# A cross-attention and feed-forward kernel: its first block in two halves, its opening reordered, the last values in row pairs

## The chip, the cores and the metric

One core of one Trainium2 chip. A core has a matrix engine (TensorE, PE in the profile, its weight loads PEld), a vector engine (VectorE, DVE), a scalar engine (ScalarE, ACT), a general engine (GpSimd, POOL), a queue engine (SyncE, SP), and 16 DMA engines that they share. Each engine works through its own instructions in the order of the program and waits for the others by semaphores. The metric is the device time of one execution, in microseconds (us).

## What is computed

x is 2048 rows of 256, the context 1601 rows of 192, all in float32. The rows of x are normalised, attend to the context with 16 heads of 64 (a learned null key and value stand ahead of the 1601), are projected back, normalised and added; then a feed-forward network of three layers with weights of +1 and -1 is added.

```python
def attention(x, context, mask):
    x = layer_norm(x, g_norm)
    q = x @ Wq
    k, v = jnp.split(context @ Wkv, 2, axis=-1)
    q, k, v = (to_heads(q), to_heads(k), to_heads(v))
    k = jnp.concatenate([nk, k], axis=2)
    v = jnp.concatenate([nv, v], axis=2)
    sim = jnp.einsum('bhid,bhjd->bhij', q * sqrt_scale, k * sqrt_scale)
    sim = jnp.where(full_mask, sim, max_neg)
    out = jnp.einsum('bhij,bhjd->bhid', softmax(sim), v)
    return layer_norm(merge_heads(out) @ Wout, g_out)

x = x + attention(_layernorm(x), ctx_768, mask)
x = x + ffn(_layernorm(x), k0, k1, k2, s0, s1, s2)
```

## The kernel before

**Tiling.** The rows of x are four blocks of 512 (b), each four tiles of 128; the heads are eight pairs (p), so that a pair fills 128 partitions. The 1602 keys are 13 tiles of 128 (KC), in four chunks for the maxima: 512, 512, 512 and 66 (CHUNKS). There are 32 units (p, b), counted u from 0. All of the program is under a manual schedule: what each engine does follows the order of the calls.

**A unit.** For each of the 13 key tiles, TensorE makes transposed scores (L442), ScalarE their exponents (L468), GpSimd adds the exponents up into acc (L720 to L728), and, for the unit after this one, TensorE makes untransposed scores (L400, L384) of which VectorE takes row maxima (L403, L387). Then come the products with the values (L475), the last unit's output projection, the queries of the unit after next (project_q), and one part of the next pair's keys (project_k, b = 0 and 1) or values (project_v, b = 2 and 3). A softmax shift, the maximum, is put into the scores by one matmul (L466) for the first two key tiles of a unit.

**Values.** A values block is up to eight key tiles in one PSUM tile of two banks, four tiles of 128 columns to a bank. values_begun (L300) multiplies the first 128 of the context's 192 rows (ctx_a), values_ended (L314) adds the other 64 (ctx_b). ctx_b and the weights wb hold these 64 rows twice, in partitions 0 to 63 and 64 to 127, so that two matmuls with 64 rows each can lie in the array at once: a tile in the first bank takes the lower rows, one in the second bank the upper. Block m = 0 holds tiles 0 to 7, block m = 1 tiles 8 to 12: 8 to 11 in the first bank, 12 in the second. values_ended goes through the tiles so that those with the same place in the two banks follow each other: 8, 12, 9, 10, 11. One ScalarE copy (L329) takes the block to SBUF. The units do project_v(p, 1) for p = 1 to 7.

**The opening** (L579 to L677), before the first unit. Transfers are issued from three queues: GpSimd's (the identity is made first, then g_norm, null keys, the mask's row `keep`), SP's and ScalarE's (x in four tiles in turns, the first context chunk on ScalarE's, the weights of pair 0 and the rest on SP's). Then block 0 is normalised whole: statistics of four tiles (L79, L80), a root on ScalarE (L535), a reciprocal (L543), four centrings (L91) on VectorE; TensorE meanwhile does eleven matmuls of the identity with itself into a spare PSUM tile (L635), which are used for nothing. It transposes the block (L556, scaled into xnT by L557 and L561), makes the first 512 keys (first_keys(0), L243 with ctx_a and L250 with ctx_b; VectorE subtracts the null key and masks them, L232, and ScalarE and GpSimd round them to kr, L258 and L260) and the queries in two halves of 256 (first_queries, L226 to L228). From there maxima of block 0 (max_chunk, twelve of 512 keys and REST for the last 66 of all four tiles), the other keys and the values of pair 0, the normalisation of block 1 (second_summed, second_normed, input_turned(1)) and its queries (project_q(0, 1)) are woven together. The opening ends with the first scores, the shifts (max_combined, max_turned) and a count of masked keys (masked_counted, L428) in front of the first L466.

PSUM is eight banks: two tiles of two banks each in a pool `flex` (ps_f) and two in a pool `spare` (ps_s). Calls for a tile take the two of a pool in turns and wait until the tile taken two calls before has been read.

**Two tiny copies** on ScalarE in each unit (`seen`, L708 and L711) read a value of the last exponents and of the last unit's acc, and so make ScalarE wait for those who write them. The second stands at step 8 of the 13, in units 3 to 27 at step 2:

```python
for k in range(KC):
    if k == (2 if 2 < u < len(units) - 4 else 8) and last is not None:
        nc.scalar.copy(seen[:, 1:2], last[3][:1, 0, 0:1])
```

Of the kernel before, what the change touches and what calls it, by code (L numbers as in the profile page):

```python
# [9 lines left out]
F32 = mybir.dt.float32  # L10
# [11 lines left out]
CD = 192  # L22
# [9 lines left out]
REST = 12  # L32
# [6 lines left out]
def xattn_ffn(ctx, tc, x, ctxT, mask, g_norm, null_kv, wq, wkv, wout, g_out, k0, k1, k2, s0, s1, s2, out):  # L39
# [55 lines left out]
    n_slots = 0  # L95
# [52 lines left out]
    with ExitStack() as att:  # L148
# [22 lines left out]
        def load_pair(p):  # L171
            wq_t = pp.tile([128, 2, 128], F32, tag="wq", name=f"wq_{p}")
            wa_t = pp.tile([128, 2, 128], F32, tag="wa", name=f"wa_{p}")
            wb_t = pp.tile([128, 2, 128], F32, tag="wb", name=f"wb_{p}")
            wo_t = lp.tile([128, D], F32, tag="wo", name=f"wo_{p}")
            both = wkv.rearrange("r (k w) -> r k w", k=2)[:, :, ts(p, 128)]
            nc.sync.dma_start(out=wa_t, in_=both[0:128])
            nc.sync.dma_start(out=wb_t[:64], in_=both[128:CD])
            nc.sync.dma_start(out=wb_t[64:], in_=both[128:CD])
            nc.sync.dma_start(out=wq_t, in_=wq[:, ts(p, 128)].rearrange("(c r) w -> r c w", c=2))  # L180
            if p > 0:
                nc.sync.dma_start(out=wo_t, in_=wout[ts(p, 128), :])
            weights[p] = (wq_t, wa_t, wb_t, wo_t)
# [32 lines left out]
        def first_queries(h):  # L216

            if h == 0:
                qT = wp.tile([128, 512], F32, tag="qT", name="qT_0_0")
                qr = wp.tile([128, 512], F32R, tag="qr", name="qr_0_0", bufs=1)  # L220
                queries[0, 0] = (qT, qr)
            qT, qr = queries[0, 0]
            ps = spare(f"psq_0_0_{h}")
            cols = ts(h, 256)
            for c in range(2):
                nc.tensor.matmul(ps[:, 0, :256], weights[0][0][:, c, :], xnT[:, 0, c, cols], start=c == 0, stop=c == 1)  # L226
            nc.scalar.mul(qr[:, cols], ps[:, 0, :256], DH**-0.5)  # L227
            nc.scalar.mul(qT[:, cols], ps[:, 0, :256], DH**-0.5)  # L228
# [5 lines left out]
        def first_keys(n, get, part=None):  # L234
# [3 lines left out]
            if part != 1:  # L238
                halves["k"] = get(f"psk_0_{n}")
# [6 lines left out]
            if part == 0:  # L246
                return
# [51 lines left out]

        def values_begun(p, m, tiles, get=flex):  # L300

            if (p, m) not in halves:
                halves[p, m] = get(f"psv_{p}_{m}").rearrange("p i (t d) -> p (i t) d", d=128)
            for t in tiles:
                nc.tensor.matmul(  # L305
                    halves[p, m][:, t - 8 * m, :],
                    ctx_a[:, ts(t, 128)],
                    weights[p][1][:, 1, :],
                    start=t % 4 == 0,
                    stop=False,  # L310
                    skip_group_check=True,
                )

        def values_ended(p, m):  # L314
# [3 lines left out]
            for t in sorted(tiles, key=lambda t: (t % 4, t)):  # L318
                rows = ts((t - 8 * m) // 4, 64)
                nc.tensor.matmul(  # L320
                    pv[:, t - 8 * m, :],
# [6 lines left out]
            w = len(tiles)  # L328
            nc.scalar.copy(v[:, ds(8 * m, w), :], pv[:, :w, :])  # L329
# [3 lines left out]
        def project_v(p, m):  # L333

            values_begun(p, m, range(8 * m, min(8 * m + 8, KC)))
            values_ended(p, m)

# [87 lines left out]
        def masked_counted(get):  # L425

            ps = get("count")
            nc.tensor.matmul(ps[:, 0, :KC], ones_r.bitcast(F32), kept, start=True, stop=True)  # L428
            nc.vector.tensor_reduce(spent, ps[:, 0, :KC], AX.X, ALU.add)
# [149 lines left out]
        nc.gpsimd.memset(keep[:, 0:1], 0)  # L579
        make_identity(nc, ident)  # L580
# [3 lines left out]
        nc.gpsimd.dma_start(out=keep[:, 1:], in_=mask.partition_broadcast(128))  # L584
        for t in range(4):
            (nc.sync, nc.scalar)[t % 2].dma_start(out=x_sb[:, t, :], in_=x[ts(t, 128), :])
        load_context(nc.scalar, 0)
        load_pair(0)
# [40 lines left out]
        xn = input_root(0)  # L629

        input_normed(0, *xn)

        idle = slot("idle")
        for _ in range(11):
            nc.tensor.matmul(idle[:, 0, :128], ident, ident, start=True, stop=True)  # L635
        input_turned(0, spare)
        first_keys(0, flex)
        first_queries(0)
        max_chunk(0, 0, 0)
        max_chunk(0, 0, 3)  # L640
        first_queries(1)
        nc.gpsimd.tensor_copy(kept[:, : KC - 1], mcol_u8[:, : KC - 1])
        nc.gpsimd.tensor_copy(kept[:KLAST, KC - 1 : KC], mcol_u8[:KLAST, KC - 1 : KC])
        mv, r = second_summed()
        max_chunk(0, 0, 6)
        first_keys(1, spare, 0)
        max_chunk(0, 0, 9)
        first_keys(1, spare, 1)
        values_begun(0, 0, range(0, 8), spare)
        max_chunk(0, 0, 1)  # L650
        nc.vector.reciprocal(r, r)
        second_normed(mv, r)
        nc.scalar.activation(warm, eps_sb, AF.Exp)
        max_chunk(0, 0, 4)
        values_ended(0, 0)
        max_chunk(0, 0, 7)
        first_keys(3, spare)
        max_chunk(0, 0, 10)
        values_begun(0, 1, range(8, KC), spare)
        max_chunk(0, 0, 2)  # L660
        values_ended(0, 1)
        max_chunk(0, 0, 5)
# [5 lines left out]
        max_chunk(0, 0, 11)  # L668
        project_q(0, 1, spare)
        max_chunk(0, 0, REST)  # L670
# [6 lines left out]
        masked_counted(flex)  # L677
        begin.__exit__(None, None, None)
        last = None
        with tc.manual_schedule():  # L680
            for u, (p, b) in enumerate(units):
# [27 lines left out]
                for k in range(KC):  # L709
                    if k == (2 if 2 < u < len(units) - 4 else 8) and last is not None:  # L710
# [243 lines left out]
```

## Time and profile before

| | us |
|---|---|
| median of 3 runs (lowest, highest) | 1270.21 (1269.99, 1270.72) |
| the profiled execution, its own time | 1270.18 |
| its span, first to last instruction | 1268.4 |
| TensorE busy | 1257.9 (99%) |
| VectorE, ScalarE, GpSimd busy | 761.7, 717.9, 1008.5 |
| opening, to the first exponent (L468) | 34.65 |
| units, from there to the last values' copy (L782) | 1079.25 - 34.65 = 1044.6 |
| feed-forward network after it | some 189 |

A profile lists what each engine did, by the line of the program that issued it. "Idle before" is the time that an engine stood still ahead of an instruction, with what released it. A matmul's end is modelled, so that those which follow each other overlap: the distance between starts tells more than the length. A float32 matmul is two instructions on TensorE. Transfers have a sequencer's time for the issue (SPq, ACTq) and a time to landing.

The engines' shares by slices of the span: TensorE is at nine tenths or more in nearly all of them, and transfers matter in the first slice alone:

```profile
PE   8999999999999999999999999999999999999998
PEld 5344444444444444444444444444444443788887
DVE  6687766656665566556655666656666793635431
ACT  4776666666666656665666566666666676322120
POOL 5898999899889988998899988998898999701100
PEclk9999999999999999999999999999999999999999
DMA  6000000000000000000000000000000010000000
```

### The profile page before, as it was taken

To read this page: it belongs to the slowest core of one execution; us is meant where nothing else is said; L and a number is where in the kernel's file an instruction comes from. 1 tells how busy PE (TensorE), PEld (TensorE's weight loads), DVE (VectorE), ACT (ScalarE), POOL (GpSimd) and SP (SyncE) were. 2 spreads that over 40 slices of the span, in tenths; PEclk is the share of its full clock that TensorE was granted. 3 is DMA by queue.
4 is the path that set the end of the run, shared out by engine and by line. 5 is a ranking of instruction groups with operands and counts; after the bars stand their busy time and mean duration, and the time that the engine had idled before them with its cause. 6 is when DMAs were issued, how large, how long until landed. Compare 5 with 4: busy or idle time off the path is not lost.

```text
span 1268.4 us, 19642 instructions
## 1 busy us (share of the span) xinstructions
PE 1257.9 (99%) x8332; PEld 644.0 (51%) x8332; DVE 761.7 (60%) x812; ACT 717.9 (57%) x982; POOL 1008.5 (80%) x515
## 2 busy tenths in 40 slices
PE   8999999999999999999999999999999999999998
PEld 5344444444444444444444444444444443788887
DVE  6687766656665566556655666656666793635431
ACT  4776666666666656665666566666666676322120
POOL 5898999899889988998899988998898999701100
PEclk9999999999999999999999999999999999999999
DMA  6000000000000000000000000000000010000000
GB/s 171 1 1 5 1 1 13 5 1 1 13 5 1 1 14 5 1 1 13 5 1 2 13 5 1 1 1 6 1 17 1 1 42 1 1 17 1 17 17 17
DMA packets 16984, 13.46 MB, mean 11 GB/s; under 512 B 3152, under 2 KB 16336, under 8 KB 16896
## 3 DMA queue, kind: packets, MB, share of 16 engines
q1 hardware_dynamic: 15904, 11.21, 3.2%
q8 instruction: 65, 1.06, 0.4%
q10 hardware_dynamic: 656, 0.79, 0.2%
q0 software_dynamic: 336, 0.21, 0.1%
q14 instruction: 23, 0.19, 0.0%
HBM read 10.11 MB, written 2.10 MB: 10 GB/s over the span
## 4 chain that ended last, share of the span: by engine, by line
PE 95%; POOL 2%; ACT 1%; DMA 1%; issue 0%; DVE 0%; SPq 0%; DVEq 0%; POOLq 0%; ACTq 0%
PE sT L442 28%; PE av L475 27%; PE ps L836 12%; PE max L400 7%; PE psq L211 4%; PE po L488 4%; PE ps L867 2%; PE psv L305 2%; PE psk L270 1%; PE den L499 1%; PE sT L466 1%; PE psv L320 1%; POOL acc L728 1%; PE psk L275 1%; PE max L384 1%; PE mt L413 1%
## 5 line engine op out<-in xcount | busy, mean ns | idle before, releaser
L403 DVE TENSOR_REDUCE mx<-max 128x2 f32<-128x1024 f32 x384 | 444.4, 1218 | 86.0 <-PE max L400 82.3
L728 POOL TENSOR_TENSOR acc<-acc,e 128x1024 f32<-128x1024 f32 x192 | 473.1, 2464 | 15.1
L468 ACT ACTIVATE e<-sT 128x1024 f32<-128x1024 f32 x416 | 425.8, 1024 | 87.7 <-PE sT L466 44.3
L442 PE MATMUL sT<-qT,kT 64*128 64x512 f32 x1664 | 444.8, 608 | 1.6 <-ACT e L468 1.3
L722 POOL TENSOR_TENSOR acc<-acc,e 128x1024 f32<-128x1024 f32 x160 | 379.3, 2371 | 12.6
L475 PE MATMUL av<-e,v 128*32 128x512 f32 x3328 | 363.6, 592 | 0.1
L400 PE MATMUL max<-kr,qr 64*128 64x512 f32 x768 | 280.6, 718 | 1.2 <-ACT qr L227 1.0
L475 PEld LDWEIGHTS av<-e,v 128*32 128x32 f32 x3328 | 107.4, 110 | 237.9 <-issue 230.1
L442 PEld LDWEIGHTS sT<-qT,kT 64*128 64x128 f32 x1664 | 134.0, 185 | 132.6 <-ACT e L468 121.0
L720 POOL TENSOR_TENSOR acc<-e,e 128x1024 f32<-128x1024 f32 x32 | 75.6, 2363 | 59.6 <-ACT e L468 59.6
L400 PEld LDWEIGHTS max<-kr,qr 64*128 64x128 f32 x768 | 76.7, 187 | 88.6 <-DVE mx L403 65.2
L517 ACT COPY aoT<-r 32x256 f32<-32x256 f32 x224 | 90.2, 403 | 33.4 <-DVE r L511 31.1
L782 ACT COPY avs<-av 128x512 f32<-128x512 f32 x32 | 18.8, 587 | 145.8 <-PE av L475 145.8
L415 DVE TENSOR_TENSOR mT<-mt,pick 128x512 fp32r<-128x512 f32 x32 | 22.1, 690 | 113.4 <-PE mt L413 112.9
L518 DVE TENSOR_TENSOR aoT<-avs,aoT 128x512 f32<-128x512 f32 x28 | 33.3, 1189 | 94.4 <-ACT aoT L517 94.4
L836 PE MATMUL ps<-h0hi,w 128*128 128x512 f32 x256 | 79.6, 392 | 0.0
L836 PE MATMUL ps<-h0lo,w 128*128 128x512 f32 x256 | 78.9, 389 | 0.0
L124 POOL TENSOR_TENSOR y_sb<-y_sb,gout_sb 128x256 f32<-128x256 f32 x12 | 9.3, 777 | 85.6 <-DVE y_sb L91 85.6
L824 ACT ACTIVATE h1hi<-ps 128x1024 fp32r<-128x1024 f32 x16 | 16.4, 1027 | 99.2 <-PE ps L836 99.2
L212 ACT ACTIVATE qr<-psq 128x512 fp32r<-128x512 f32 x31 | 18.5, 598 | 93.5 <-PE psq L211 91.4
L488 PE MATMUL po<-wo,aoT 128*128 128x256 f32 x256 | 60.5, 379 | 0.0
L825 DVE SCALAR_TENSOR_TENSOR h1lo<-ps,h1hi 128x1024 fp32r<-128x1024 f32 x16 | 19.6, 1224 | 67.0 <-ACT h1hi L824 67.0
(171 smaller groups left out, 1207.8 us busy)
## 6 DMA issues: line engine op xcount, KB each, us to landing
out_x<-o SPq DMA_DIRECT2D x7, 256.0 KB, 2.1
x_sb<-in_x SPq DMA_DIRECT2D x3, 512.0 KB, 5.2
wa<-in_wkv SPq DMA_DIRECT2D x8, 128.0 KB, 2.9
wb<-in_wkv SPq DMA_DIRECT2D x16, 64.0 KB, 2.5
wq<-in_wq SPq DMA_DIRECT2D x8, 128.0 KB, 2.2
wo<-in_wout SPq DMA_DIRECT2D x8, 128.0 KB, 2.1
xnT<-in_k SPq DMA_DIRECT2D x1, 1024.0 KB, 5.7
ctx_a<-in_ctxT SPq DMA_DIRECT2D x2, 256.0 KB, 6.2
```

Of the source, the lines that this page charges most:

```text
L211: nc.tensor.matmul(ps[:, 0, :], weights[p][0][:, c, :], xnT[:, b, c, :], start=c == 0, stop=c == 1)
L400: nc.tensor.matmul(ps[:, j, :w], qr[rows, ts(t, 128)], kr[rows, ds(start, w)], start=True, stop=True)
L403: nc.vector.tensor_reduce(maxima[p, b][:, t, :, c], ps[:, :, :w], AX.X, ALU.max)
L442: nc.tensor.matmul(ps[:n, j, :], kT[rows, ds(128 * KEY_TILES[k], n)], qT[rows, :], start=k < 2, stop=k >= 2, skip_group_check=k >= 2,)
L468: nc.scalar.activation(e, ps, AF.Exp)
L475: nc.tensor.matmul(av[ts(i, 32), 0, :], v[:n, KEY_TILES[k], ts(i, 32)], e[:n, i // 2, :], start=k == 1, stop=k == 0, tile_position=(0, 32 ...
L488: nc.tensor.matmul(pv[:, t, :], aoT[:, ts(t, 128)], weights[p][3], start=True, stop=True)
L517: nc.scalar.copy(aoT[ds(64 * j + 32 * rows, 32), ts(h, 256)], r[ds(64 * j + 32 * h, 32), :])
L720: nc.gpsimd.tensor_tensor(acc, es[1], es[2], ALU.add)
L722: nc.gpsimd.tensor_tensor(acc, acc, es[k], ALU.add)
L728: nc.gpsimd.tensor_tensor(acc, acc, es[k], ALU.add)
L836: nc.tensor.matmul(ps[:, f, :], w(c)[:, ts(2 * g + f, 128)], parts[part][:, c, :], start=i == 0, stop=i == len(steps) - 1,)
```

## The change

1. The opening's transfers: on GpSimd's queue g_norm and the null keys go ahead of the identity; `keep` moves to SP's queue. x's first two tiles are issued first, then the first weights (wa), the first context chunk (ScalarE's queue), `keep`, wb's lower half, wq, x's other two tiles (the fourth on ScalarE's queue), wb's upper half.
2. Block 0 is normalised in two halves of two tiles (first_stats, first_centred, first_turned). Three identity matmuls instead of eleven stand ahead; the first part of the first keys stands before the transposes of the first half; the statistics of the second half stand after the first queries and its centrings after the first maximum's reduction. Eight identity matmuls stand between the second maximum and the second half's transposes, in the unused bank of the first queries' tile.
3. The second part of the opening: the first part of chunk 1's keys goes ahead of the third maximum, the values' parts are split around the maxima, REST goes ahead of project_q(0, 1), the count of masked keys goes from the end to after the last keys, into a bank of their tile.
4. Values block m = 1 puts tiles 8 to 10 into the first bank and 11 and 12 into the second; values_ended then goes 8, 11, 9, 12, 10. Its copy becomes two, of three and of two tiles.
5. The second `seen` copy stands at step 2 in unit 28 too.

n_slots starts at 1 because the empty matmuls no longer take a tile by turns; the tiles of later blocks stay the same.

```diff
-        def load_pair(p):
+        def load_pair(p, part=None):
+            if part == 1:
+                ...
+                nc.sync.dma_start(out=wb_t[:64], in_=both[128:CD])
+                nc.sync.dma_start(out=wq_t, in_=wq[:, ts(p, 128)].rearrange("(c r) w -> r c w", c=2))
+                return
+            if part == 2:
+                ...
+                nc.sync.dma_start(out=weights[p][2][64:], in_=both[128:CD])
+                return
...
+        places = {t: t if t < 8 else t - 8 if t < 11 else t - 7 for t in range(KC)}
...
-                    halves[p, m][:, t - 8 * m, :],
+                    halves[p, m][:, places[t], :],
...
-                    start=t % 4 == 0,
+                    start=places[t] % 4 == 0,
...
-            for t in sorted(tiles, key=lambda t: (t % 4, t)):
-                rows = ts((t - 8 * m) // 4, 64)
+            for t in sorted(tiles, key=lambda t: (places[t] % 4, t)):
+                rows = ts(places[t] // 4, 64)
...
-            w = len(tiles)
-            nc.scalar.copy(v[:, ds(8 * m, w), :], pv[:, :w, :])
+            for at, w in ((0, 8),) if m == 0 else ((8, 3), (11, 2)):
+                nc.scalar.copy(v[:, ds(at, w), :], pv[:, ds(places[at], w), :])
...
+        def first_stats(h):
+            mv = stats(x_sb[:, ts(h, 2), :], 2, f"x0{h}")
+            r = sp.tile([128, 4], F32, tag="rstd", name=f"rstd_x0{h}")
+            nc.scalar.activation(r[:, :2], mv[:, :2, 1], AF.Sqrt, bias=eps2_sb, scale=1.0 + EPS)
+            return h, mv, r
+        def first_centred(h, mv, r):
+            nc.vector.reciprocal(r[:, :2], r[:, :2])
+            for j in range(2):
+                centred(y_sb[:, 2 * h + j, :], x_sb[:, 2 * h + j, :], mv, r, j)
+        def first_turned(h):
+            pt = spare(f"xT_0_{h}")
+            cols = ts(h, 256)
+            for j in range(2):
+                for c in range(2):
+                    nc.tensor.transpose(pt[:, c, ts(j, 128)], y_sb[:, 2 * h + j, ts(c, 128)], ident)
+            nc.scalar.mul(xnT[:, 0, 0, cols], pt[:, 0, :256], gn_sb[:, 0:1])
+            if h == 0:
+                nc.vector.tensor_scalar_mul(xnT[:, 0, 1, cols], pt[:, 1, :256], gn_sb[:, 1:2])
+            else:
+                nc.scalar.mul(xnT[:, 0, 1, cols], pt[:, 1, :256], gn_sb[:, 1:2])
...
-        nc.gpsimd.memset(keep[:, 0:1], 0)
-        make_identity(nc, ident)
         nc.gpsimd.dma_start(out=gn_sb, in_=g_norm.rearrange("(c p) -> p c", p=128))
         for j in range(2):
             nc.gpsimd.dma_start(out=nullk[ts(j, DH), :], in_=null_kv[0].rearrange("(p o) -> p o", o=1))
-        nc.gpsimd.dma_start(out=keep[:, 1:], in_=mask.partition_broadcast(128))
-        for t in range(4):
-            (nc.sync, nc.scalar)[t % 2].dma_start(out=x_sb[:, t, :], in_=x[ts(t, 128), :])
+        nc.gpsimd.memset(keep[:, 0:1], 0)
+        make_identity(nc, ident)
+        for t, engine in enumerate((nc.sync, nc.scalar)):
+            engine.dma_start(out=x_sb[:, t, :], in_=x[ts(t, 128), :])
+        load_pair(0, 0)
         load_context(nc.scalar, 0)
-        load_pair(0)
+        nc.sync.dma_start(out=keep[:, 1:], in_=mask.partition_broadcast(128))
+        load_pair(0, 1)
+        for t, engine in ((2, nc.sync), (3, nc.scalar)):
+            engine.dma_start(out=x_sb[:, t, :], in_=x[ts(t, 128), :])
+        load_pair(0, 2)
...
-        xn = input_root(0)
-        input_normed(0, *xn)
-        idle = slot("idle")
-        for _ in range(11):
+        idle = flex("idle")
+        for _ in range(3):
             nc.tensor.matmul(idle[:, 0, :128], ident, ident, start=True, stop=True)
-        input_turned(0, spare)
-        first_keys(0, flex)
+        first_centred(*first_stats(0))
+        first_keys(0, flex, 0)
+        first_turned(0)
+        first_keys(0, flex, 2)
         first_queries(0)
+        later = first_stats(1)
         max_chunk(0, 0, 0)
+        first_centred(*later)
         max_chunk(0, 0, 3)
+        for _ in range(8):
+            nc.tensor.matmul(halves["q0"][:, 1, :128], ident, ident, start=True, stop=True)
+        first_turned(1)
         first_queries(1)
...
+        first_keys(1, spare, 0)
         mv, r = second_summed()
         max_chunk(0, 0, 6)
-        first_keys(1, spare, 0)
+        first_keys(1, spare, 1)
         max_chunk(0, 0, 9)
-        first_keys(1, spare, 1)
-        values_begun(0, 0, range(0, 8), spare)
+        first_keys(1, spare, 2)
+        values_begun(0, 0, range(0, 6), spare)
         max_chunk(0, 0, 1)
+        values_begun(0, 0, range(6, 8), spare)
+        max_chunk(0, 0, 4)
         nc.vector.reciprocal(r, r)
         second_normed(mv, r)
+        values_ended(0, 0)
         nc.scalar.activation(warm, eps_sb, AF.Exp)
-        max_chunk(0, 0, 4)
-        values_ended(0, 0)
         max_chunk(0, 0, 7)
         first_keys(3, spare)
+        masked_counted(halves["k"])
         max_chunk(0, 0, 10)
+        max_chunk(0, 0, 2)
         values_begun(0, 1, range(8, KC), spare)
-        max_chunk(0, 0, 2)
+        max_chunk(0, 0, 5)
         values_ended(0, 1)
-        max_chunk(0, 0, 5)
...
+        max_chunk(0, 0, REST)
         project_q(0, 1, spare)
-        max_chunk(0, 0, REST)
...
-        masked_counted(flex)
...
-                    if k == (2 if 2 < u < len(units) - 4 else 8) and last is not None:
+                    if k == (2 if 2 < u < len(units) - 3 else 8) and last is not None:
```

More of the change, by code (lines that the diff above doesn't have):

```diff
@@ L94, in xattn_ffn @@
     norms = {}
-    n_slots = 0
+    n_slots = 1
     def slot(name):
@@ L169, in xattn_ffn @@
         weights = {}
-        def load_pair(p):
+        def load_pair(p, part=None):
+            if part == 1:
+                wq_t, wa_t, wb_t, wo_t = weights[p]
+                both = wkv.rearrange("r (k w) -> r k w", k=2)[:, :, ts(p, 128)]
+                nc.sync.dma_start(out=wb_t[:64], in_=both[128:CD])
+                nc.sync.dma_start(out=wq_t, in_=wq[:, ts(p, 128)].rearrange("(c r) w -> r c w", c=2))
+                return
+            if part == 2:
+                both = wkv.rearrange("r (k w) -> r k w", k=2)[:, :, ts(p, 128)]
+                nc.sync.dma_start(out=weights[p][2][64:], in_=both[128:CD])
+                return
             wq_t = pp.tile([128, 2, 128], F32, tag="wq", name=f"wq_{p}")
@@ L177, in load_pair @@
             nc.sync.dma_start(out=wa_t, in_=both[0:128])
+            if part == 0:
+                weights[p] = (wq_t, wa_t, wb_t, wo_t)
+                return
             nc.sync.dma_start(out=wb_t[:64], in_=both[128:CD])
@@ L222, in first_queries @@
             qT, qr = queries[0, 0]
-            ps = spare(f"psq_0_0_{h}")
+            ps = halves[f"q{h}"] = spare(f"psq_0_0_{h}")
             cols = ts(h, 256)
@@ L237, in first_keys @@
             chunks = (CHUNKS[1], CHUNKS[2]) if n == 1 else (CHUNKS[n],)
-            if part != 1:
+            if not part:
                 halves["k"] = get(f"psk_0_{n}")
@@ L245, in first_keys @@
                     )
-            if part == 0:
+            if part in (0, 1):
                 return
@@ L317, in values_ended @@
             tiles = range(8 * m, min(8 * m + 8, KC))
-            for t in sorted(tiles, key=lambda t: (t % 4, t)):
-                rows = ts((t - 8 * m) // 4, 64)
+            for t in sorted(tiles, key=lambda t: (places[t] % 4, t)):
+                rows = ts(places[t] // 4, 64)
                 nc.tensor.matmul(
-                    pv[:, t - 8 * m, :],
+                    pv[:, places[t], :],
                     ctx_b[rows, ts(t, 128)],
@@ L423, in rows_of, with masked_counted @@
             return 128
[L425 to L429, printed above, removed]
+        def masked_counted(ps):
+            nc.tensor.matmul(ps[:, 1, :KC], ones_r.bitcast(F32), kept, start=True, stop=True)
+            nc.vector.tensor_reduce(spent, ps[:, 1, :KC], AX.X, ALU.add)
             nc.gpsimd.tensor_scalar(spent, spent, float(KEYS), ident[:, KLAST : KLAST + 1], ALU.subtract, ALU.mult)
```

## The prediction, made before the result was known

> **What bounds the kernel now.** I read the chain of waits first, then the opening instruction by instruction, the waits of the transfer queues, and last the stretch of one unit's score loop.
>
> The chain's shares by engine:
>
> ```profile
> PE 95%; POOL 2%; ACT 1%; DMA 1%; issue 0%; DVE 0%; SPq 0%; DVEq 0%; POOLq 0%; ACTq 0%
> ```
>
> TensorE sets the end nearly everywhere, so an edit is worth what it takes from TensorE's line or from the waits on it. The units repeat; the opening, up to the first matmul of the shifts (L466, 34.11 us), is the one stretch where TensorE waits for inputs. Timeline of TensorE there (start, length, line, shapes, count, idle before and its releaser):
>
> ```profile
> 1.38 4.20 PE L635 MATMUL idle<-ident 128*128 128x128 f32 x22 [1.38 <-POOL ident masks.py:199]
> 6.71 1.43 PE L556 MATMUL xT<-ident,y_sb 128*128 128x128 f32 x8 [1.14 <-DVE y_sb L91]
> 8.12 1.10 PE L243 MATMUL psk<-ctx_a,wa 128*128 128x512 f32 x2
> 9.14 1.12 PE L250 MATMUL psk<-ctx_b,wb 64*128 64x512 f32 x2
> 10.20 1.13 PE L226 MATMUL psq<-xnT,wq 128*128 128x256 f32 x4
> 11.89 0.73 PE L400 MATMUL max<-kr,qr 64*128 64x512 f32 x4 [0.56 <-ACT qr L227]
> 12.56 1.13 PE L226 MATMUL psq<-xnT,wq 128*128 128x256 f32 x4
> 14.16 0.50 PE L400 MATMUL max<-kr,qr 64*128 64x512 f32 x2 [0.47 <-ACT qr L227]
> ...
> 22.00 0.49 PE L400 MATMUL max<-kr,qr 64*128 64x512 f32 x2 [0.20 <-DVE mx L403]
> ...
> 24.03 1.38 PE L305 MATMUL psv<-wa,ctx_a 128*128 128x128 f32 x10 [0.33 <-ACT v L329]
> ...
> 32.50 0.30 PE L413 MATMUL mt<-ident,mcol 128*128 128x128 f32 x1 [0.26 <-DVE mcol L408]
> ...
> 34.11 0.50 PE L466 MATMUL sT<-mT,ones_r 64*128 64x512 f32 x2
> ```
>
> From the second half of the queries (12.56) to L466 it is 21.55 us, of which the bracketed waits make 0.47 + 0.20 + 0.33 + 0.26 = 1.26: 20.3 us is work. VectorE runs close behind: its maxima go from 12.43 to 32.05, 1.17 to 1.22 us each.
>
> **The change, part by part. Transfers.** The queue's waits in the first 30 us:
>
> ```profile
> SPq L591 <- DMA ctx_a<-in_ctxT: 1.4, 1, 1.4
> ...
> SPq L179 <- DMA x_sb<-in_x: 0.6, 1, 0.6
> ```
>
> L179 is the ninth transfer of the two hardware queues in program order and is issued only at 3.62, when the first x tile has landed (3.44, when VectorE takes it up); L591, the thirteenth, waits for the fifth. So eight are in flight. In the new order x's third tile is the ninth and the fourth, on ScalarE's queue, the tenth: it is issued near 3.6, and behind it in ScalarE's order stand its 0.45 us of issue, the table load (1.28, now at 2.70), the warm root (0.20) and the root that the first half waits for. That root moves to 3.6 + 0.45 + 1.28 + 0.25 = 5.6, where VectorE's statistics of two tiles would have allowed 4.65. Then root 0.30, reciprocal 0.18, two centrings (0.35 apart, 0.41 long), hand-overs of 0.03: the first half stands at 6.9, against 7.64 for all four tiles before. The early tiles gain little.
>
> On GpSimd's queue the norm's scale and the two null keys go ahead of the identity: 0.98 + 1.08 of issue, so the identity comes at about 3.4 instead of 1.32. Only the matmuls that compute nothing wait for it. The mask's row leaves GpSimd for SP, ahead of wb and wq, 0.5 us of issue; it lands well before its first use (issued 1.8, 5.2 to landing, used after 9). The later chunks' issues shift by about a microsecond; the first is needed at 15.4 and landed at 10.8.
>
> **First keys.** Their first part now stands ahead of the transposes and waits for wa (landed 7.98) and ctx_a (7.25). Both are issued 0.5 earlier, with 256 KB less ahead, 1.1 us at the 230 GB/s of those slices: 5.7 to 6.4; I take 5.9, with bounds 5.3 and 7.5 (issue alone). How fast they then run depends on TensorE's pace. The windows of half a microsecond show it (elapsed, then busy time and count of TensorE, its loads, VectorE, ScalarE, GpSimd; clock, transfer share, GB/s):
>
> ```profile
> 3.50:4.00 0.50, 0.50 (x4) 0.50 (x4) 0.47 (x3) 0.49 (x2) 0.50 (x2) 1.00 1.20 323
> ...
> 4.50:5.00 0.50, 0.50 (x7) 0.50 (x6) 0.47 (x3) 0.00 (x0) 0.50 (x2) 1.00 0.80 215
> ```
>
> The 22 empty matmuls start 0.21 us apart until about 4.4 and 0.11 after it, at a granted clock of 1.00 throughout: the first three microseconds run at half pace. Now six run from 3.4 to 4.8, then TensorE idles for a microsecond. Warm, the two key matmuls take 1.06; at half pace 2.1. I take 1.6: 7.5. Four transposes at the later block's 1.09 for eight: 8.05. Second part of the keys 1.06: 9.1. Queries there, and the first maximum's matmul 1.69 after them as now (10.20 to 11.89): 10.8; its reduction 0.54 later: 11.35. Now it is 12.43: 1.1 us won.
>
> [...]
>
> **Second half.** Its reciprocal and centrings stand behind that reduction on VectorE: 11.35 + 1.22 + 1.0 = 13.57; transposes and the scaling, as y's end to xnT now (0.43 + 0.38 + 0.03), 14.4. Its statistics (four instructions, 1.04) fit under the first queries. So the second queries start at 14.4, not 12.56. The eight matmuls between the halves, 16 x 0.11 = 1.7 us warm, fill TensorE from 11.4 to 13.1, where it waits for these tiles anyway; with that cover gone they would cost 1.7, and at half pace 3.4.
>
> **From there to L466.** The work is the same 20.3 us, less 0.22 for one values block (below): moving the count, the statistics or the splits takes nothing off TensorE. The 0.47 goes, since a key matmul now stands between queries and maximum. New waits: the first maximum of chunk 1 stands behind a reduction, the key subtraction (0.75) and GpSimd's copy (0.62), 0.35; another buffer 0.2; and the last maximum, now ahead of the second block's queries, needs the buffer of the one two before it, which VectorE frees 0.95 after TensorE gets there. Before, 1.96 us of queries covered that. Behind it queue these queries and both first scores, 4.1 us, which hold L466. Sum 20.1 + 1.5 = 21.6; L466 at 36.0 instead of 34.11: a loss of 1.9. Bounds: first half at 6.9, keys warm and done before it, no new wait, 13.65 + 20.1 = 33.75, a gain of 0.36; keys at 7.5 at half pace, 16.5 + 21.6 = 38.1, a loss of 4.0.
>
> **Values in row pairs.** Second parts of the two values blocks in the units:
>
> ```profile
> 925.36 1.16 PE L320 MATMUL psv<-wb,ctx_b 64*128 64x128 f32 x16
> ...
> 958.20 1.04 PE L320 MATMUL psv<-wb,ctx_b 64*128 64x128 f32 x9
> ...
> 959.09 0.27 PE L320 MATMUL psv<-wb,ctx_b 64*128 64x128 f32 x1
> ```
>
> Sixteen instructions, four pairs in different rows, have the same 0.89 us from first to last start as ten, one pair and three singles. A pair costs what a single does, 0.22; two pairs and a single cost three of them. That is 0.22 less on TensorE in seven units: 1.55. ScalarE's copy becomes two, 0.49 + 0.39 by the slope of its 0.99 (1024) and 0.69 (640), 0.1 overlapped, 0.1 more in all; the exponent behind it now waits 0.25 for TensorE, which covers it. Bounds 0 to 0.33 each.
>
> **The acc copy in unit 28.** Score loops of units 24 and 28:
>
> ```profile
> 828.49:843.43 14.94, 14.94 (x98) 7.25 (x98) 14.22 (x13) 13.40 (x15) 12.55 (x6) 1.00 0.00 1
> 960.55:975.89 15.34, 15.26 (x98) 7.31 (x98) 14.42 (x13) 13.28 (x15) 12.64 (x6) 1.00 0.00 1
> ```
>
> The same loop takes 0.40 longer with ScalarE's look at acc at step 8 than at step 2. GpSimd has that acc at 961.95 and step 2 comes at 962.73, so the wait is covered by 0.78 and the 0.40 are won; bounds 0 and 0.45.
>
> **Sum.** +1.9 - 1.55 - 0.40 = -0.05 on the profiled execution's own 1270.18 (span 1268.4): 1270.1, the median being 1270.21.
>
> **The rivals.** A, the forecast, chance 0.38: the opening loses about what the units win. Own range 1267.9 to 1272.2, from the opening's bounds.
>
> B, chance 0.36: the opening wins too. For it: its 512-wide matmuls start 0.53 apart (8.12, 8.62, 9.14), in the units 0.43 (L211, four in 1.88); if steadier work brings some ten of them to that pace, 1.0 goes, and if VectorE's earlier start removes the new waits, 1.5. 36.0 - 2.5 = 33.5, 0.6 won, with the units 2.55: 1267.6; 1266.9 if the first half is at its bound (13.65) as well, 1266.1 with the pairs at 0.33. Against it: the second queries cannot start before 13.65.
>
> C, chance 0.22, slower: half pace up to the second half. The two key parts and the queries then cost 1.06 more each and the empty matmuls between the halves 1.7, less the 0.5 already counted: 4.4 more, 1274.5; partly so, 1273. It decides once more than 2.6 us of this holds. For it the rows above; against it that 5.9 to 9 is nearly all work.
>
> D, chance 0.04: the pairs do not overlap, because passes of one tile follow each other; 1.55 falls away, 1271.7.
>
> **How the numbers follow.** Time 1270.1. Range 1266.2 to 1273.4: it holds A and D, nearly all of B and the nearer part of C. 0.2% is 2.5 us, about what a measurement of this kernel can tell from no change. Faster 0.36 (B), same 0.42 (A, D), slower 0.22 (C).
>
> **What would show it.** Right: the root of the first half near 5.6 behind the table load; first reduction near 11.4, second queries near 14.4; a TensorE wait for VectorE ahead of L384; L466 near 36; seven values blocks 0.22 shorter, unit 28's loop at 14.94. Wrong: second queries before 13.5 (B), empty matmuls and key matmuls 0.21 and 1.06 apart past 8 us (C), an L320 block that still spans 0.89 (D).

## The result, and the profile after

The changed kernel is slower: 1274.38 us median (1270.80 to 1277.94, 22 executions) against 1270.30 (1269.87 to 1271.93, 22 executions), ratio 1.0029 with a 95% interval of 1.0020 to 1.0037. The prediction, 1270.1 with a range of 1266.2 to 1273.4, was wrong.

The median alone misleads here. The 22 times lie in two groups: ten at 1270.80 to 1272.51, twelve at 1274.07 to 1277.94, and nothing between. The kernel before has no second group in these 22 executions (1269.87 to 1271.93). So two things are to be explained: a loss of a good microsecond in the lower group, and three to six more in half of the executions. The profiled execution took 1271.49 (span 1269.7): it shows the first. What shows the second is among the experiments.

Timeline of TensorE in the opening of the changed kernel (start, length, line, shapes, count, idle before and its releaser). L256 and L263 are the keys with ctx_a and ctx_b, L372 the transposes of a half, L239 the queries, L441 the maxima, L425 REST, L468 the count, L506 the shifts (L466 before):

```profile
4.02 1.65 PE L675 MATMUL idle<-ident 128*128 128x128 f32 x6 [4.02 <-POOL mcol_u L655]
6.00 2.05 PE L256 MATMUL psk<-ctx_a,wa 128*128 128x512 f32 x2 [0.33 <-DMA wa<-in_wkv]
7.83 1.06 PE L372 MATMUL xT<-ident,y_sb 128*128 128x128 f32 x4
8.83 1.12 PE L263 MATMUL psk<-ctx_b,wb 64*128 64x512 f32 x2
...
11.57 0.74 PE L441 MATMUL max<-kr,qr 64*128 64x512 f32 x4 [0.57 <-POOL kept L689]
12.24 2.05 PE L686 MATMUL psq<-ident 128*128 128x128 f32 x16
14.13 0.60 PE L372 MATMUL xT<-ident,y_sb 128*128 128x128 f32 x4
15.29 1.13 PE L239 MATMUL psq<-xnT,wq 128*128 128x256 f32 x4 [0.56 <-ACT xnT L373]
...
21.85 0.50 PE L441 MATMUL max<-kr,qr 64*128 64x512 f32 x2 [0.26 <-POOL kr L273]
...
26.19 0.39 PE L468 MATMUL psk<-kept,ones_r 128*128 128x13 f32 x2 [0.91 <-DVE kT L245]
...
32.52 0.64 PE L425 MATMUL max<-kr,qr 64*128 64x66 f32 x8 [1.18 <-DVE mx L444]
...
37.24 0.50 PE L506 MATMUL sT<-mT,ones_r 64*128 64x512 f32 x2
```

The shifts come at 37.24 instead of 34.11: the opening lost 3.13. Of this 2.73 are there when the second queries start (15.29, before 12.56); from them to the shifts it is 21.95 instead of 21.55, with waits of 0.26, 0.91 and 1.18. The first three rows show half pace, which means that matmuls of one kind start twice as far apart as later on: the first keys take 1.83 from start to start, four transposes 1.00, where the second part of the keys right behind them takes 1.05 (8.83 to 9.88).

The score loop of unit 28 (window, elapsed, busy time and count of TensorE, its loads, VectorE, ScalarE, GpSimd, clock, transfer share, GB/s):

```profile
962.22:977.16 14.94, 14.94 (x98) 7.24 (x98) 14.22 (x13) 13.38 (x15) 12.79 (x6) 1.00 0.00 1
```

It begins 1.67 later than before (960.55), so of the 3.13 seven values blocks have won back 1.46, 0.21 each; and it takes 14.94 instead of 15.34, which wins another 0.40. 3.13 - 1.46 - 0.40 = 1.27, which is the difference of the two spans (1.3).

Three more rows: a wait of SP's queue, then the issue of x's fourth tile on ScalarE's queue and the root of the first half on ScalarE:

```profile
SPq L628 <- POOL ident masks.py:197: 1.1, 1, 1.1
```

```profile
2.23 0.59 ACTq L631 DMA_DIRECT2D x_sb<-in_x  x1
4.44 0.30 ACT L357 ACTIVATE rstd_x<-mv_x,eps_sb 128x2 f32<-128x2 f32 x1
```

The first is the issue of the mask's row. It stands on SP's queue now, but the tile is partly written by a memset on GpSimd, which stands behind the issues of g_norm and the null keys; SP waits for it until 3.49, with wb, wq and x's third tile queued behind. The root is at 4.44: x's fourth transfer was issued at 2.23 without any wait.

### The profile page after: what moved, and what is told of

Same layout as the page of the kernel before. It is cut to its first block, busy times and chain, and to the rows that moved or that the text cites. A ratio compares the mean times of both kernels' runs of the same rounds, so it can differ in the third digit from the quotient of the medians.

```text
span 1269.7 us, 19654 instructions
## 1 busy us (share of the span) xinstructions
PE 1255.6 (99%) x8332; PEld 642.3 (51%) x8332; DVE 758.8 (60%) x813; ACT 719.1 (57%) x993; POOL 1007.4 (79%) x514
## 3 DMA queue, kind: packets, MB, share of 16 engines
q8 instruction: 65, 1.06, 0.4%
## 4 chain that ended last, share of the span: by engine, by line
PE 92%; POOL 5%; issue 1%; DVE 1%; ACT 0%; DVEq 0%; POOLq 0%; ACTq 0%
PE sT L482 27%; PE av L515 26%; PE ps L885 12%; PE max L441 7%; PE psq L224 4%; PE po L528 4%; PE ps L916 2%; POOL acc L777 2%; POOL acc L771 2%; PE psv L320 2%; PE psk L283 1%; PE den L539 1%; PE sT L506 1%; PE psv L335 1%; PE psk L288 1%
## 5 line engine op out<-in xcount | busy, mean ns | idle before, releaser
L777 POOL TENSOR_TENSOR acc<-acc,e 128x1024 f32<-128x1024 f32 x192 | 473.3, 2465 | 15.1
L441 PE MATMUL max<-kr,qr 64*128 64x512 f32 x768 | 280.4, 718 | 0.8 <-POOL kept L689 0.6
L441 PEld LDWEIGHTS max<-kr,qr 64*128 64x128 f32 x768 | 76.5, 187 | 88.2 <-DVE mx L444 65.2
```

The source lines that it names most:

```text
L441: nc.tensor.matmul(ps[:, j, :w], qr[rows, ts(t, 128)], kr[rows, ds(start, w)], start=True, stop=True)
L777: nc.gpsimd.tensor_tensor(acc, acc, es[k], ALU.add)
```

## The experiments

Theory: half pace of TensorE early in the opening makes the upper group, since three empty matmuls do not bring it to full pace (the first keys behind them take 1.83) and eleven do (1.02 in the kernel before, 8.12 to 9.14). Rivals: the transfers in their new order; the order of the second part; the halves themselves. All kernels were timed beside the kernel before (its medians were 1270.33, 1270.50 and 1270.42). "Upper" counts the executions more than 2.5 us above the kernel's own lowest. By this count 9 of the 99 executions of the kernel before that were timed beside these are upper, too (5 of 35, 3 of 35, 1 of 29), the highest at 1274.33.

| kernel | lowest, median, highest us | ratio to before (95%) | upper |
|---|---|---|---|
| again | 1271.02, 1272.06, 1278.96 | 1.0024 (1.0011 to 1.0037) | 5 of 12 |
| units_only | 1267.89, 1268.73, 1270.80 | 0.9985 (0.9976 to 0.9993) | 1 of 11 |
| three | 1268.73, 1272.11, 1276.27 | 1.0013 (0.9998 to 1.0027) | 6 of 12 |
| warm | 1270.88, 1272.60, 1274.28 | 1.0012 (1.0003 to 1.0020) | 1 of 11 |
| tail | 1269.93, 1270.86, 1274.68 | 1.0012 (1.0002 to 1.0021) | 5 of 11 |
| warm_tail | 1270.10, 1270.37, 1271.16 | 1.0000 (0.9992 to 1.0009) | 0 of 11 |
| no_fill | 1273.45, 1274.40, 1278.30 | 1.0034 (1.0022 to 1.0046) | 1 of 6 |
| front_only | 1270.56, 1273.96, 1275.86 | 1.0020 (1.0010 to 1.0030) | 6 of 11 |
| second_only | 1268.83, 1269.19, 1273.07 | 0.9994 (0.9986 to 1.0003) | 1 of 11 |
| keep_back | 1268.93, 1269.81, 1270.48 | 0.9995 (0.9987 to 1.0004) | 0 of 11 |
| repaired | 1269.06, 1269.70, 1270.30 | 0.9993 (0.9985 to 1.0002) | 0 of 11 |
| best | 1267.89, 1268.47, 1271.46 | 0.9981 (0.9973 to 0.9990) | 1 of 11 |

**again**: the changed kernel, without an edit.

> The changed kernel as it is, to see its spread within one chip and, with luck, a profile of one of its long executions (its 22 times lie in two clusters, 1270.8 to 1272.5 and 1274.1 to 1277.9). Theory P (pace): in the long executions TensorE goes on at half pace beyond 9 us, so the trace shows the first keys' second part, the queries or the eight empty matmuls at double spacing (1.06 and 0.21 us) and L506 at 41 to 43 instead of 37.2. Rival T (transfers): the pace is the same and an opening transfer lands 3 to 6 us later. Rival U (units): L506 stays at 37.2 and the time goes in the units. Times: about half of them at 1271 to 1272.5, the rest at 1274 to 1278.

The two groups came again, seven executions at 1271.02 to 1272.21 and five at 1274.60 and above. This time the profiled execution (1274.60) is of the upper group. Its timeline of TensorE, then windows of one microsecond (columns as above, the clock third from the end):

```profile
9.17 1.12 PE L263 MATMUL psk<-ctx_b,wb 64*128 64x512 f32 x2 [1.25 <-DMA wb<-in_wkv]
10.22 1.45 PE L239 MATMUL psq<-xnT,wq 128*128 128x256 f32 x4
...
13.38 3.79 PE L686 MATMUL psq<-ident 128*128 128x128 f32 x16
16.96 0.98 PE L372 MATMUL xT<-ident,y_sb 128*128 128x128 f32 x4
...
40.45 0.50 PE L506 MATMUL sT<-mT,ones_r 64*128 64x512 f32 x2
```

```profile
9.00:10.00 1.00, 0.83 (x2) 0.29 (x2) 0.00 (x0) 0.00 (x0) 0.00 (x0) 1.00 0.93 169
...
11.00:12.00 1.00, 0.67 (x2) 0.00 (x0) 0.97 (x4) 0.60 (x3) 0.67 (x3) 0.50 1.08 258
...
17.00:18.00 1.00, 0.94 (x5) 0.62 (x3) 0.00 (x0) 0.02 (x1) 0.00 (x0) 0.64 1.10 325
```

The second part of the keys still runs at full pace (9.17 to 10.22). But after its 1.25 of waiting for wb the granted clock falls to 0.50 near 10.9 and stays there to about 17.7. The empty matmuls between the halves need 3.58 (13.38 to 16.96) instead of 1.89, now on the path: VectorE had the second half ready at 15.1. The shifts come at 40.45. So it is the pace that is lost, but here a late transfer came ahead of the loss. This execution is the lowest of the upper group; of those above it none was profiled.

**units_only**: the kernel before with the row pairs and unit 28 alone.

```diff
 (before)
+        places = {t: t if t < 8 else t - 8 if t < 11 else t - 7 for t in range(KC)}
...
-                if k == (2 if 2 < u < len(units) - 4 else 8) and last is not None:
+                if k == (2 if 2 < u < len(units) - 3 else 8) and last is not None:
```

> The kernel before with two parts of the change alone: the row pairs of the last values and the acc copy at step 2 of unit 28; the opening as before. All theories but U: the opening at 34.1, seven values blocks 0.21 shorter, unit 28's loop 14.94 instead of 15.34, so 1270.2 - 1.5 - 0.4 - 0.2 (the block of the opening) = 1268.1 to 1268.4, and no second cluster. Theory U: no gain, or a second cluster of times.

Median 1268.73, nine of eleven at 1267.89 to 1268.92: 1.6 less than before by medians, where 1.8 to 2.1 were expected. These parts hold nearly what was forecast of them, and all of the loss is in the opening. The profiled execution is the longest (1270.80) and shows that the opening of before, with its eleven empty matmuls, can lose its pace too. Behind waits of 0.48 and 0.58 the granted clock is at 0.50 from 26.2 to 29.6:

```profile
24.16 0.51 PE L402 MATMUL max<-kr,qr 64*128 64x512 f32 x2 [0.48 <-DVE mx L405]
25.25 1.68 PE L307 MATMUL psv<-wa,ctx_a 128*128 128x128 f32 x10 [0.58 <-ACT v L331]
```

**three**: units_only with three empty matmuls instead of eleven, and no other edit.

```diff
-        for _ in range(11):
+        for _ in range(3):
             nc.tensor.matmul(idle[:, 0, :128], ident, ident, start=True, stop=True)
```

> The kernel before with the two parts in the units (row pairs, unit 28), whose median was 1268.73 with 9 of 11 executions at 1267.9 to 1268.9, and with three empty matmuls ahead of the opening instead of eleven; nothing else of the opening is changed. Pace theory (the empty matmuls are what brings TensorE to full pace before the opening's real work): the six instructions end before 2.7 us, the eight transposes (1.43 before) take over 1.7, the first key parts some 2.1 each instead of 1.06 to 1.12, and about half of the executions keep the half pace longer; a second group of times appears 3 to 6 us above the first, the first group is 1 to 2 us above 1268.3, median 1270 to 1273. Rival (the second group comes from the halves and the new order of transfers, not from the pace at the start): one group at 1268 to 1269, median within 0.5 us of 1268.7.

Two groups: six executions at 1268.73 to 1269.66, six at 1274.56 to 1276.27. This one number, in an opening otherwise as before, makes the upper group, some 6 us above the lower. Its profiled execution, one of the lower group (1269.22):

```profile
1.38 1.65 PE L637 MATMUL idle<-ident 128*128 128x128 f32 x6 [1.38 <-POOL ident masks.py:199]
6.75 1.97 PE L558 MATMUL xT<-ident,y_sb 128*128 128x128 f32 x8 [3.72 <-DVE y_sb L91]
8.51 1.92 PE L243 MATMUL psk<-ctx_a,wa 128*128 128x512 f32 x2
10.35 1.20 PE L250 MATMUL psk<-ctx_b,wb 64*128 64x512 f32 x2
```

Transposes and first keys at half pace until 10.3: 0.8 lost, as the lower groups say (1268.73 against 1267.89). Of the upper group no execution of this kernel was profiled.

**warm**: the changed kernel with the identity ahead of g_norm and the null keys, and thirteen empty matmuls.

```diff
+        nc.gpsimd.memset(keep[:, 0:1], 0)
+        make_identity(nc, ident)
         nc.gpsimd.dma_start(out=gn_sb, in_=g_norm.rearrange("(c p) -> p c", p=128))
...
-        nc.gpsimd.memset(keep[:, 0:1], 0)
-        make_identity(nc, ident)
...
-        for _ in range(3):
+        for _ in range(13):
```

> The change with the identity first on GpSimd's queue again (ahead of the norm's scale and the null keys) and 13 empty matmuls ahead instead of 3, so that TensorE is busy from 1.4 to about 6. Theory P: the first keys take 1.06 instead of 1.83, the four transposes 0.6 instead of 1.0, the first reduction starts near 10.9 instead of 12.1, L506 at about 36.0 instead of 37.2, and the second cluster is gone: 1270.0 to 1270.5 in all executions. Theory T: both clusters stay, both some 1.2 lower at most. Theory U: no change.

The expected 1270.0 to 1270.5 did not come. One execution is left above 1273.1, but eight of the eleven lie at 1272.42 or above. The profiled one (1273.09):

```profile
8.58 1.09 PE L263 MATMUL psk<-ctx_b,wb 64*128 64x512 f32 x2 [0.50 <-DMA wb<-in_wkv]
9.99 1.10 PE L239 MATMUL psq<-xnT,wq 128*128 128x256 f32 x4 [0.31 <-DMA wq<-in_wq]
...
32.60 0.64 PE L425 MATMUL max<-kr,qr 64*128 64x66 f32 x8 [1.18 <-DVE mx L444]
33.16 3.57 PE L224 MATMUL psq<-xnT,wq 128*128 128x512 f32 x4
```

At full pace TensorE reaches wb and wq before they have landed: the first maximum comes at 11.65, no earlier than 11.57. And behind the wait of 1.18 ahead of REST the queries take 3.57 instead of 1.98, at a granted clock of 0.50. There are two occasions of half pace, one early in the opening and one late. The edit also brings the memset of the mask's tile ahead, so that SP issues the mask's row at 1.90 instead of 3.49: it changes the transfers as well, which three does not.

**tail**: the changed kernel with REST behind project_q(0, 1) and the count at the end, as before.

```diff
-        masked_counted(halves["k"])
...
-        max_chunk(0, 0, REST)
         project_q(0, 1, spare)
+        max_chunk(0, 0, REST)
...
+        masked_counted(flex("count"))
```

> The change with the last maximum behind the second block's queries again and the count at the end of the opening again, all else as changed. The theory of new waits (0.91 for the count behind VectorE's key subtraction, 1.18 for the last maximum's buffer): these waits go, the count's 0.32 comes back at the end, and L506 is at 35.5 to 36.3 instead of 37.2, so the short executions fall to 1270 to 1270.7. If VectorE sets the end anyway, only 0.3 is won. Theory P expects the second cluster to stay, 3 to 6 us above the first.

The lower group falls by a good microsecond, to 1269.93 to 1270.86. The upper one stays: it begins a microsecond lower than in again and ends four lower, 1273.59 to 1274.68. Its profiled execution (1273.88):

```profile
8.77 2.07 PE L263 MATMUL psk<-ctx_b,wb 64*128 64x512 f32 x2
10.77 2.07 PE L239 MATMUL psq<-xnT,wq 128*128 128x256 f32 x4
13.41 1.22 PE L441 MATMUL max<-kr,qr 64*128 64x512 f32 x4 [0.56 <-ACT qr L240]
14.56 3.39 PE L686 MATMUL psq<-ident 128*128 128x128 f32 x16
```

Here the half pace of the start has not ended: every kind of matmul takes about twice its time until about 17.4. The clock column shows 1.00 through all of this, as it did for the first three microseconds of before; over the half pace that came behind full pace in again it shows 0.50. So half pace is read from the starts of the matmuls, not from this column alone.

**warm_tail**: the changed kernel with the edits of warm and of tail, both shown above.

> The changed kernel with two repairs at once: the identity ahead of g_norm and the null keys with thirteen empty matmuls instead of three, and REST behind the second block's queries and the count at the end, as before. Alone, the first left a group of times at 1272.4 to 1273.1 (half pace behind the 1.18 of wait ahead of REST), the second left one at 1273.6 to 1274.7 (half pace from the start). Pace theory: each repair takes away one of the two occasions of half pace, so one group remains, at 1269.9 to 1270.9, and median near 1270.3. Rival (the groups come from something else, such as the transfers in the new order): two groups again, the upper at 1272 or above with a third of the executions or more.

One group, 1270.10 to 1271.16. Each edit removed its occasion. Together with three, where the number of empty matmuls alone makes the upper group, this shows pace as its cause; this is the time of the kernel before, with the units' gain eaten by the rest of the opening.

**no_fill**: the changed kernel without the eight empty matmuls between the halves.

```diff
-        for _ in range(8):
+        for _ in range(0):
             nc.tensor.matmul(halves["q0"][:, 1, :128], ident, ident, start=True, stop=True)
```

> The changed kernel without the eight empty matmuls between the halves; nothing else is changed. The prediction priced them at nothing, under the wait for the second half's tiles, and at 1.7 to 3.4 where that cover is gone. At half pace they took 3.79 (12.23 to about 16). If they are covered in the short executions and on the path in the long ones: the short group stays at 1271.0 to 1271.5, the long group falls from 1274.6 to 1279 to some 1273 to 1275. Rival (they hold the pace for what follows): the transposes and queries of the second half and the keys behind them run at half pace in most executions, median 1 us or more above the changed kernel's 1272.

All six executions are at 1273.45 or above. The profiled one (1274.37):

```profile
13.57 0.76 PE L372 MATMUL xT<-ident,y_sb 128*128 128x128 f32 x4 [1.61 <-DVE y_sb L91]
14.89 2.05 PE L239 MATMUL psq<-xnT,wq 128*128 128x256 f32 x4 [0.56 <-ACT xnT L373]
16.74 1.83 PE L256 MATMUL psk<-ctx_a,wa 128*128 128x512 f32 x2
```

The wait of 1.61 stands where the empty matmuls were, and behind it queries and keys run at half pace (granted clock 0.50 from 14.9 to 18.3). So the expected stay of the lower group was wrong and the rival right. At full pace these matmuls cost next to nothing: the second queries start 3.72 behind the first maximum with them (11.57 to 15.29 in the profiled execution of the changed kernel), 3.66 without (11.23 to 14.89). And they hold it: with them the granted clock stayed at 1.00 there from 12 to 18.

**front_only** and **second_only** part the opening in two. The first is the changed kernel with the second part of before; the second is units_only with the new second part (keys, values, maxima, count and REST as in point 3 of the change). The core of the first edit; the second is its reverse in the other kernel:

```diff
-        first_keys(1, spare, 0)
         mv, r = second_summed()
         max_chunk(0, 0, 6)
+        first_keys(1, spare, 0)
...
-        masked_counted(halves["k"])
...
-        max_chunk(0, 0, REST)
         project_q(0, 1, spare)
+        max_chunk(0, 0, REST)
...
+        masked_counted(flex)
```

> The changed kernel with the second part of the opening in the order of before (chunk 1's keys, the values' parts, REST behind the second block's queries, the count of masked keys at the end); transfers, halves, three and eight empty matmuls, row pairs and unit 28 stay changed. If the loss sits in the first part (half pace and the transfers): short executions near 1270, the second group of times 3 to 5 us above them stays, median 1270.5 to 1274, as with REST and the count alone undone (1270.86). If the interleaving of keys, values and maxima makes the loss: one group at or below 1268.7.

> The kernel before with row pairs and unit 28 (1268.73), and with the second part of the opening in the new order, REST ahead of the second block's queries and the count behind the last keys; the first part and the transfers are those of before. By the changed kernel's waits of 0.91 ahead of the count and 1.18 ahead of REST, less the 0.47 that the key matmul covers: shifts of the first unit 1 to 2 us later than 34.1, times 1269.5 to 1270.7 and few at 1274 or above. If the new order was bad only because the new first part leaves VectorE behind: the waits vanish, times 1268 to 1268.8.

The new front alone has the upper group (six of eleven at 1273.96 to 1275.86) and a lower group from 1270.56, 2.7 above the lowest of units_only. The profiled execution of the first (1273.96, in the upper group) is at half pace up to about 17, as tail's. The new second part alone costs 0.46 by medians, less than the expected 1 to 2, and 0.94 between the lowest. It brings the two waits even with the old front, in the profiled execution (1273.07) with half pace behind each:

```profile
24.58 0.39 PE L429 MATMUL psk<-kept,ones_r 128*128 128x13 f32 x2 [0.92 <-DVE kT L232]
...
32.46 0.64 PE L386 MATMUL max<-kr,qr 64*128 64x66 f32 x8 [1.18 <-DVE mx L405]
33.02 3.62 PE L211 MATMUL psq<-xnT,wq 128*128 128x512 f32 x4
```

**keep_back**: warm_tail with the mask's row back on GpSimd's queue.

```diff
+        nc.gpsimd.dma_start(out=keep[:, 1:], in_=mask.partition_broadcast(128))
...
-        nc.sync.dma_start(out=keep[:, 1:], in_=mask.partition_broadcast(128))
```

> The kernel with both repairs, and the mask's row back on GpSimd's queue behind the null keys, so that on SP's queue wb's lower half and wq follow wa at once. In the changed kernel with full pace at the start, the first half waited 0.50 for wb and 0.31 for wq and had its first maximum at 11.65. If the transfers bound the first half: these waits shrink by 0.6 (one issue and 200 KB less ahead of them), the first maximum near 11.0 and the times 0.5 to 0.8 below the kernel with both repairs. Rival (the row's 200 KB share the same 16 engines whatever the queue, or the second half's x is late then): no change, within 0.3.

Median 1269.81, 0.56 below warm_tail. The first maximum of warm_tail, then of keep_back:

```profile
8.98 1.09 PE L263 MATMUL psk<-ctx_b,wb 64*128 64x512 f32 x2 [0.47 <-DMA wb<-in_wkv]
...
11.84 0.74 PE L441 MATMUL max<-kr,qr 64*128 64x512 f32 x4 [0.57 <-POOL kept L690]
```

```profile
8.29 1.12 PE L263 MATMUL psk<-ctx_b,wb 64*128 64x512 f32 x2
...
11.03 0.73 PE L441 MATMUL max<-kr,qr 64*128 64x512 f32 x4 [0.56 <-ACT qr L240]
```

The wait for wb is gone and the maximum is 0.81 earlier: with pace mended, the transfers bounded the first half. The wait for the memset is not what this prices, since it is gone in warm_tail already.

**best** and **repaired**: best is units_only with the count moved from the end to behind the first part of the last values block, in the second bank of the last keys' tile. repaired has the same second part, but the halves, with the edits of warm and of keep_back shown above; against best it prices the halves with their order of x's and the weights' transfers, and thirteen empty matmuls ahead instead of eleven.

```diff
 (best, beside units_only)
         values_begun(0, 1, range(8, KC), spare)
+        masked_counted(halves["k"])
...
-        masked_counted(flex)
```

> The kernel before with row pairs and unit 28 (1268.73) and the count of masked keys moved from the end of the opening to behind the first part of the last values block, two steps later than in the changed kernel, into the second bank of the last keys' tile. VectorE has subtracted the null key from that tile by then, so the 0.91 of wait should not come back, and the buffer that the count took at the end comes free: 1268.0 to 1268.7. Rival: the count's reduction, moved among the maxima, delays VectorE, which runs close behind there: 0.2 to 0.5 later, 1269.0.

> Block 0 in halves with everything else put back or mended: identity first, thirteen empty matmuls, the mask's row on GpSimd's queue, the second part of the opening in the order of before with the count behind the first part of the last values block, row pairs and unit 28. Beside the best kernel so far (1268.47, the same with block 0 whole) it prices the halves themselves. If the halves win once pace and transfers are mended: 1267 to 1268. If the second half's reciprocal, centrings and transposes behind the first reduction cost more than the earlier first maximum brings: 1268.9 to 1270, in one group of times.

best is the fastest kernel, 1268.47, some 2 us below the kernel before; from units_only (1268.73) it can't be told apart. repaired has one group at 1269.70: the halves cost 1.2 even with everything else mended. VectorE in repaired:

```profile
11.85 1.23 DVE L444 TENSOR_REDUCE mx<-max 128x2 f32<-128x1024 f32 x1
...
13.18 0.74 DVE L91 TENSOR_SCALAR y_sb<-x_sb,mv_x,rstd_x 128x256 f32<-128x256 f32 x2
13.83 1.22 DVE L444 TENSOR_REDUCE mx<-max 128x2 f32<-128x1024 f32 x1
17.17 1.23 DVE L444 TENSOR_REDUCE mx<-max 128x2 f32<-128x1024 f32 x1 [2.12 <-PE max L441]
```

and in best:

```profile
12.56 3.50 DVE L405 TENSOR_REDUCE mx<-max 128x2 f32<-128x1024 f32 x3 [1.19 <-PE max L402]
```

The first reduction is 0.71 earlier, but the second half is centred only behind it, at 13.9; its queries start at 15.03 instead of 12.69, and the third reduction at 17.17 instead of some 14.9. Shifts at 35.80 against 34.19.

## Why the prediction was wrong, point by point

**Pace: the step that failed.** The prediction gave the first keys 1.6 (between 1.06 and 2.1), let the half pace end there, and kept "half pace up to the second half" as case C at 0.22, priced 1274.5. In the lower group the keys took 1.83 and the transposes 1.00 instead of 0.55, and in half of the executions, 12 of 22 at 1274.07 to 1277.94, the price was that of C. None of the twelve was profiled; the long executions that were, with the same start, were at half pace up to the second half (tail to 17.4, front_only to about 17) or got there a second time (again, 10.9 to 17.7). The mechanism, its place and its price were named; its chance was too small. The argument set against it, that from 5.9 to 9 TensorE is nearly all at work, was no reason: tail worked from 5.89 on with one wait of 0.56 and stayed at half pace to 17.4. The price was also a little low (the middle of the twelve is 1276.3). C left out the transposes of the first half and the first maximum, which cost 0.5 more each in tail, and it counted one stretch from the start and no second one behind a wait (again); how the longest executions come about was not seen.

**Transfers.** The root at 5.6, behind a blocked x transfer, was wrong: 4.44. The eight in flight of the prediction's rows are not refuted by this: SP's queue stood still behind the memset, so fewer than eight were out ahead of x's fourth transfer at 2.23. In repaired, where the mask's row is not on SP's queue and x's fourth transfer is the ninth in the program, VectorE takes up x's first tile at 3.41 and waits 1.07 for the root ahead of its reciprocal at 5.66 (L362); with the 0.33 from root to reciprocal before (5.70 to 6.03) the root is estimated at 5.3, close to what was predicted. The early root gave nothing, for the keys waited for wa (0.33) and half pace set the rest. The mask's row was taken to cost SP 0.5 of issue; it cost a wait of 1.1 on GpSimd's memset, and without that wait its place on SP's queue still cost 0.56 (keep_back against warm_tail). That wb and wq could be late was not considered.

**First and second half.** First reduction 12.11 instead of 11.35, from the pace. From it to the second queries 3.18, predicted 3.05: right. The empty matmuls between the halves: 0.06 at full pace, priced at nothing; that they hold the pace (no_fill) was not seen.

**From there to the shifts.** 21.95, predicted 21.6. The total was nearly right, the waits not: REST's was 1.18 (0.95 predicted), chunk 1's 0.26 (0.35), and the count's 0.91 was missed. The count writes into the tile of the last keys, and so has to wait until VectorE has subtracted the null key there, which stands behind the maxima. tail, without both, is 1.1 faster by the lowest (1269.93 against again's 1271.02).

**Units.** Row pairs 0.21 a block (0.22), unit 28 0.40 (0.40); units_only 1.6 by medians against 1.95. Right in the rows, a little less in the times.

**The sum.** In the profiled execution of the lower group the opening lost 3.13 instead of 1.9, of which 0.76 stands ahead of the first reduction; the loss of a microsecond there is this. The median is 1274.38 because twelve of the 22 executions lose nearly five more (1276.3 against 1271.4 between the middles of the groups). Which group holds the median is chance: in again, the same kernel, five of twelve were long, and the median, 1272.06, lay inside the predicted range.

## What to carry to other kernels

Matmuls that compute nothing can be load-bearing (without the eight between the halves the lowest time was 1273.45, with them 1270.80): before cutting them, ask whether the matrix engine is at full pace without them, and count not one execution but many, since the price may fall in half of them only (34 of 68 behind six instructions). Work split to start earlier gains nothing while weights that come later bound it (the wait of 0.47 for wb in warm_tail; without it, in keep_back, the first maximum is 0.81 earlier), and its later half then stands behind the first half's consumers on a shared engine (centred only at 13.9 in repaired, and 1.2 slower than best). A transfer into a tile that another engine partly fills moves that engine's queue into its own (here SP's wait of 1.1).

## What the runs showed of the hardware that was not expected

- Kernels whose empty matmuls ahead are six instructions have the upper group in 34 of 68 executions (after, again, tail, three, front_only), those with 22 or 26 in 4 of 77 (the other seven but no_fill), and the kernel before, with 22, in 9 of its 121.
- Half pace came behind short waits: those of 1.61 and 0.91 (no_fill), 1.25 (again), 1.18 (warm, second_only), 0.92 (second_only) and 0.48 with 0.58 (units_only) were each followed, 0.8 to 1.8 us after their end, by a granted clock of 0.50. It lasted 3.4 us each time, in again 6.8, twice as long. In the profiled execution of the changed kernel the same 0.91 and 1.18 were not followed by half pace; what decides it stays open.
- Half pace after the start lasted to 8.8 us in the profiled execution of the changed kernel and to 17.4 in tail's, which does the same work up to there (three, with another opening: 10.3); why was not settled either.
